# The last product of a ternary feed forward: float32 operands replaced by two float32r halves

## The chip, the cores and the metric

The kernel runs on one NeuronCore of a Trainium2 chip. The time is the device time of one execution in microseconds (us). Before the change three executions took 3924.77, 3930.02 and 3933.33 us; the median is 3930.02 us. The engines are named as in the profile: PE (TensorE, matrix products; PEld are its weight loads), DVE (VectorE), ACT (ScalarE), POOL (GpSimd) and SP, which issues DMAs.

## The reference

The kernel computes a decoder of four layers, each an attention, a second attention and a feed forward, with a layer normalisation after each, on 16 sequences of 128 tokens and width 256. The change touches one of the twelve stages, the feed forward of the third layer:

```python
def ternary_matmul(x, w):
    return jnp.matmul(x, jnp.sign(w).T)
xq = activation_quant(rms_norm(x))
g = jax.nn.silu(ternary_matmul(xq, W_g))
u = ternary_matmul(xq, W_u)
p = g * u
return ternary_matmul(p, W_d)
```

The hidden width is 1024. Only the signs of the weights enter, so each is -1, 0 or 1. The quantised input is a small integer and is exact in bfloat16. The gated values `p` are general float32 numbers; the product of `p` with the signs of `W_d` (the down product) is what changes. The stage before it (stage 7) is an attention without weights between the tokens and a context of the same sequence.

## The kernel before

The activations stay in the core's on-chip memory (`X`, 128 tokens by 16 sequences by 256). Stage 7 and stage 8 run woven into one another. `s7` makes 16 attention units, one for a sequence (`width_unit`), and 8 feed-forward pairs, one for two sequences (`s8_pair`). Both are generators, cut into pieces at each `yield`. `weave` goes through steps n and in each calls, in a fixed list, the next piece of the unit of sequence n - lag. In the list, A is the attention unit and B the pair:

```python
(A, 0), (A, 4), (A, 1), (A, 3), (A, 1), (A, 3), (A, 2), (A, 4), (B, 11), (B, 7),
(B, 8), (B, 6), (A, 1), (B, 5), (B, 9), (A, 2), (B, 13),
```

A pair belongs to two sequences and is called for both, so it advances 14 pieces: the statistics of `X` (on DVE, then `rs_ve` and `ln_rs` on POOL), the variance and normalisation, the quantisation, the transposes, four pieces with two chunks of 128 hidden columns each (c = 0, 2, 4, 6), two pieces with the down product of one sequence (j = 0 and j = 1), the statistics of the output, its normalisation on POOL, and its transposes. Worked out from the list: in an odd step come, in this order, the statistics of the output of the pair before, the transposes of the next pair, chunks 6 of a pair, chunks 0 of the next pair, the third piece of an attention unit (`xp`), the input statistics of the pair after next, and then the down product of j = 0. The attention piece with the products `xp,e` and the exponentials `e` follows it. In an even step come chunks 2 and 4 of one pair and the down product of j = 1 of the pair before it.

`Ordered` wraps the four compute engines while the stages are woven: each instruction is held behind the one that the code put before it on the same engine. So every engine's queue has the order of the list, and an instruction that waits holds all that stands behind it on its engine. All these instructions are recorded with the one line 324; they are told apart by their tiles.

A piece of two chunks makes eight bfloat16 products of the signs `sgu` with the quantised input `qT` into two banks, multiplies the gate's bank by the row scales (`t`, DVE), applies silu (`t`, ACT) and multiplies by the other bank (`h`, DVE). The buffer `hT` (tag `h8`, line 2153) holds the eight chunks of a pair in float32 and has two copies, since the next pair begins its chunks before the down product of this pair is done. The down product of j takes, for c from 0 to 7, the 128x128 block of `hT` as weights and the signs `d` of `W_d` (128x256, float32) as the moving side. Its result is scaled and added to `X` on DVE (`X<-bankB,rs,X`).

The banks of TensorE's results come from two rotating pools in this stage: six for the wide ones (`bankA`) and two for the others (`bankB`). ACT changes its function table between silu and the exponentials, once each way in a step (ACT_TABLE_LOAD).

Of the kernel before, what the change touches and what calls it, by code (L numbers as in the profile page):

```python
# [11 lines left out]

F32 = mybir.dt.float32
BF16 = mybir.dt.bfloat16
I32 = mybir.dt.int32
AF = mybir.ActivationFunctionType
ALU = mybir.AluOpType
# [5 lines left out]
D = 256  # L23
# [245 lines left out]
def bc(ap, *shape):  # L269
    return ap.to_broadcast(list(shape))  # L270
# [56 lines left out]
class Decoder:  # L327
# [47 lines left out]
    def setup(self):  # L375
# [15 lines left out]
        self.spare = self.const(base, "spare", nc.scalar)  # L391
        self.identb = base.tile([128, 128], BF16, name="identb")
        nc.vector.tensor_copy(self.identb, self.ident)
# [1236 lines left out]
    def w5(self, pool):  # L1630
        nc = self.nc
        w = {"gu_i": pool.tile([128, 2, 2, 704], I32, name="gu5i")}
        nc.sync.dma_start(w["gu_i"], self.a["s5_wgu"].rearrange("(k p) m h -> p k m h", p=128))
        w["d_i"] = pool.tile([128, 6, D], I32, name="d5i")
        nc.sync.dma_start(
# [63 lines left out]
    def s6(self, wk, w, last):  # L1699
        nc = self.nc  # L1700
        one = dict(bufs=1)
        w["neg"] = wk.tile([128, 128], BF16, name="neg6", **one)
        nc.vector.tensor_copy(w["neg"], w["neg_causal"])
# [372 lines left out]
    def quantise(self, wk, src, tag):  # L2076
# [8 lines left out]
        nc.vector.tensor_scalar(s, s, 127.0, None, ALU.mult)  # L2085
        q = wk.tile([128, n, m], BF16, tag="q" + tag, name="q" + tag)
        for j in range(n):
# [5 lines left out]
    def s8_signs(self, wk, w):  # L2093
        w["s"] = wk.tile([128, 2, 2, 1024], BF16, name="sgu8", bufs=1)
        self.nc.scalar.activation(w["s"], w["gu"], AF.Sign)
        self.nc.scalar.activation(w["d"], w["d"], AF.Sign)

    def s8(self, wk, w, last):

# [7 lines left out]
    def s8_pair(self, wk, w, b, last, norm=True):  # L2107

        nc = self.nc
        xs = self.X[:, b : b + 2, :]
        mv, rstd = self.moments([xs[:, j, :] for j in range(2)], 1e-5 if norm else 1e-8, "ln")
        yield
        var = self.sm(2, tag="var8")
        if norm:
            nc.gpsimd.tensor_tensor(var, mv[:, :2, 1], rstd[:, :2], ALU.mult)
            nc.gpsimd.tensor_tensor(var, var, rstd[:, :2], ALU.mult)
            self.rsqrt(var, var, 1e-8, 2)
            xh = xs  # L2120
        else:
            nc.gpsimd.memset(var, 1.0)
            xh = wk.tile([128, 2, D], F32, tag="xh8", name="xh8", bufs=1)
        for j in range(2):
            nc.vector.tensor_scalar(
                xh[:, j, :], xs[:, j, :], mv[:, j, 0:1], rstd[:, j : j + 1], ALU.subtract, ALU.mult
            )
        yield
        am, s, rs = (self.sm(2, tag=n + "8") for n in ("am", "s", "rs"))
        nc.vector.tensor_reduce(am, xh, AX.X, ALU.max, apply_absolute_value=True)  # L2130
        nc.vector.reciprocal(s, am)
        nc.vector.tensor_scalar(s, s, 127.0, None, ALU.mult)
        q = wk.tile([128, 2, D], BF16, tag="q8", name="q8", bufs=1)
        t = wk.tile([128, 2, D], F32, tag="t8", name="t8", bufs=1)
        for j in range(2):
            nc.vector.tensor_scalar(t[:, j, :], xh[:, j, :], s[:, j : j + 1], MAGIC, ALU.mult, ALU.add)
            nc.gpsimd.tensor_scalar(q[:, j, :], t[:, j, :], MAGIC, None, ALU.subtract)
        nc.gpsimd.tensor_scalar(am, am, 1.0 / 127.0, None, ALU.mult)
        nc.gpsimd.tensor_tensor(rs, am, var, ALU.mult)
        yield  # L2140
        p = self.pt(2, 2, 128, dtype=BF16)
        for j in range(2):
            for k in range(2):
                nc.tensor.transpose(p[:, k, j, :], q[:, j, 128 * k : 128 * k + 128], self.identb)
        qT = wk.tile([128, 2, 256], BF16, tag="qT8", name="qT8")
        nc.scalar.copy(qT, p.rearrange("p k j t -> p k (j t)"))
        p = self.pt(2, 128)
        for j in range(2):
            self.mm(p[:, j, :], bc(rs[:, j : j + 1], 128, 128), self.ident)
        rsb = wk.tile([128, 256], F32, tag="rsb8", name="rsb8")  # L2150
        nc.scalar.copy(rsb, p.rearrange("p j t -> p (j t)"))
        yield
        hT = wk.tile([128, 8, 256], F32, tag="h8", name="h8")
        for c in range(0, 8, 2):
            ps = [self.ps(2, 256) for _ in range(2)]
            for m in range(2):
                for i in range(2):
                    cs = slice(128 * (c + i), 128 * (c + i) + 128)
                    for k in range(2):
                        self.mm(ps[m][:, i, :], w["s"][:, k, m, cs], qT[:, k, :], k, 2)  # L2160
            t = wk.tile([128, 2, 256], F32, tag="t28", name="t28")
            nc.vector.tensor_tensor(t, ps[0], bc(rsb.unsqueeze(1), 128, 2, 256), ALU.mult)
            nc.scalar.activation(t, t, AF.Silu)
            nc.vector.tensor_tensor(hT[:, c : c + 2, :], ps[1], t, ALU.mult)
            yield
        for j in range(2):
            p = self.pt(D)
            for c in range(8):
                self.mm(p, hT[:, c, 128 * j : 128 * j + 128], w["d"][:, c, :], c, 8)
            nc.vector.scalar_tensor_tensor(  # L2170
                xs[:, j, :], p, rs[:, j : j + 1], xs[:, j, :], ALU.mult, ALU.add
            )
            yield
        mv, rstd = self.moments([xs[:, j, :] for j in range(2)], 1e-5, "ln")
        yield
        for j in range(2):
            nc.gpsimd.tensor_scalar(
                xs[:, j, :], xs[:, j, :], mv[:, j, 0:1], rstd[:, j : j + 1], ALU.subtract, ALU.mult
            )
        if last:  # L2180
            nc.sync.dma_start(self.out.rearrange("b s d -> s b d")[:, b : b + 2, :], xs)
        else:
            yield
            self.load_transposed(b // 4, [b // 2 % 2])
# [399 lines left out]
```

## Time and profile before

| | |
|---|---|
| median of three executions | 3930.02 us |
| span of the profiled execution, first to last instruction | 3927.2 us |
| the profiled execution's own time outside the span | not on the page; the median stands 2.8 us above the span |
| PE busy in the span | 3561.2 us (91%) |
| DVE, ACT, POOL busy | 2528.1 us (64%), 2076.7 us (53%), 1965.7 us (50%) |
| stretch of stages 7 and 8 | about 2362 to 2665 us, 303 us |
| PE, DVE, ACT, POOL busy in that stretch | 263.9, 191.0, 145.5, 112.0 us |
| mean granted TensorE clock over the span | 0.950 |

Busy times are unions of the recorded durations. A matrix product is recorded longer than the distance to the next one, because products overlap in the array; the distance between starts tells what one costs in a row of them. A float32 product is recorded as two MATMUL instructions, a bfloat16 product as one. `[1.42 <-DVE t L324]` behind a line says that the engine was idle for 1.42 us before it and that the instruction that wrote `t` on DVE ended the wait.

### The profile page before, as it was taken

How to read it: one execution, taken by the hardware profiler on the slowest of the kernel's cores; microseconds unless marked ns; L12 is line 12 of the kernel's file. 1: busy time of each engine (PE TensorE's matmuls, PEld its weight loads, DVE VectorE, ACT ScalarE, POOL GpSimd, SP SyncE). 2: the span in 40 equal slices, each digit the busy share in tenths (PEclk: the TensorE clock that was granted, in tenths of full speed). 3: DMA queues.
4: the chain of work that ended last, by engine and by line, in shares of the span. 5: the costliest groups of instructions: out<-in, count | busy, mean ns of one | idle time of the engine just before them, and what ended most of it. 6: DMA issues, size and time to landing. Idle time of an engine off the chain costs nothing.

```text
span 3927.2 us, 96527 instructions
## 1 busy us (share of the span) xinstructions
PE 3561.2 (91%) x39282; PEld 2164.1 (55%) x39282; DVE 2528.1 (64%) x5489; ACT 2076.7 (53%) x4583; POOL 1965.7 (50%) x2227
## 2 busy tenths in 40 slices
PE   6999999999999837798989998988999999999896
PEld 4666566666666524565545664665455454555453
DVE  3776667768767565566235556755666677666697
ACT  2666666666666513343115444544656565566386
POOL 1444444435434316652125552343886666676567
PEclk8999999999999968899979998998999999999898
DMA  2111111111111101100010003111111111111221
GB/s 88 35 38 37 35 37 38 36 36 37 37 35 33 37 0 47 42 12 16 1 57 30 27 24 110 52 48 46 36 42 37 36 42 36 41 38 40 74 68 33
DMA packets 120841, 156.47 MB, mean 40 GB/s; under 512 B 15632, under 2 KB 79888, under 8 KB 120016
## 3 DMA queue, kind: packets, MB, share of 16 engines
q1 hardware_dynamic: 114544, 143.59, 12.0%
q8 instruction: 311, 5.10, 0.6%
q10 hardware_dynamic: 5712, 5.19, 0.4%
q0 software_dynamic: 144, 1.52, 0.1%
q14 instruction: 130, 1.06, 0.1%
HBM read 131.64 MB, written 2.10 MB: 34 GB/s over the span
## 4 chain that ended last, share of the span: by engine, by line
PE 73%; DVE 12%; ACT 6%; POOL 5%; issue 3%; DMA 1%; SPq 0%; ACTq 0%; POOLq 0%; DVEq 0%
PE bankA L324 39%; PE bankB L324 20%; PE bankC L324 8%; PE bankA L465 3%; DVE npad L324 2%; PE bankB L465 2%; ACT accq L324 1%; ACT ot L324 1%; ACT gT L324 1%; POOL var L324 1%; DVE X L324 1%; DVE ln_st L324 1%; POOL t L324 1%; DVE t L324 0%; DVE accq L324 0%
## 5 line engine op out<-in xcount | busy, mean ns | idle before, releaser
L324 PE MATMUL bankA<-xT,wzx 128*128 128x512 f32 x1024 | 458.1, 600 | 0.0
L324 DVE SCALAR_TENSOR_TENSOR acc<-bankA,half,acc 128x508 f32<-128x508 f32 (+2 forms) x384 | 285.2, 743 | 167.2 <-ACT acc L324 158.2
L324 POOL TENSOR_TENSOR m<-m,gm 128x512 f32<-128x512 f32 x256 | 317.9, 1277 | 48.0 <-ACT m L324 48.0
L324 PEld LDWEIGHTS bankA<-xT,wzx 128*128 128x128 f32 x1024 | 190.1, 191 | 226.6 <-issue 188.4
L324 POOL TENSOR_TENSOR eb<-eb,c_tri_s 128x512 f32<-128x512 f32 x64 | 81.2, 1269 | 371.5 <-ACT eb L324 371.5
L324 POOL TENSOR_TENSOR gT<-yx,sz 128x512 f32<-128x512 f32 x128 | 160.5, 1275 | 211.4 <-DVE yx L324 211.4
L324 PE MATMUL bankA<-xT,wkq 128*128 128x512 f32 x512 | 259.1, 631 | 0.0
L324 PE MATMUL bankA<-xT,wvg 128*128 128x512 f32 x512 | 247.5, 606 | 0.1
L324 PE MATMUL bankC<-gT,wo 128*128 128x512 f32 x512 | 231.9, 596 | 2.7 <-POOL gT L324 2.7
L324 DVE TENSOR_REDUCE npad<-bankA 128x2 f32<-128x512 f32 (+1 forms) x320 | 196.9, 681 | 37.6 <-PE bankA L324 29.0
L324 ACT ACTIVATE m<-bankA 128x512 f32<-128x512 f32 x256 | 132.1, 604 | 157.4 <-PE bankA L324 157.4
L324 ACT ACTIVATE e<-bankA 128x512 f32<-128x512 f32 x320 | 165.2, 603 | 82.2 <-PE bankA L324 81.7
L324 POOL TENSOR_TENSOR sq<-sq,s 128x512 f32<-128x512 f32 x124 | 157.5, 1271 | 56.6 <-ACT s L324 51.9
L324 POOL TENSOR_SCALAR rs_ve<-o_mv 128x4 f32<-128x4 f32 x64 | 31.5, 492 | 298.9 <-DVE o_mv L324 289.6
L324 DVE SCALAR_TENSOR_TENSOR vT<-th,accv 128x512 f32<-128x512 f32 x64 | 45.4, 710 | 182.1 <-ACT th L324 182.1
L324 PEld LDWEIGHTS bankB<-y,tt 32*32 32x32 f32 x8192 | 87.5, 107 | 129.1 <-issue 93.7
L324 DVE SCALAR_TENSOR_TENSOR yx<-xs,cols,bankB 128x512 f32<-128x512 f32 x128 | 95.0, 747 | 90.2 <-PE bankB L324 84.5
L324 DVE SCALAR_TENSOR_TENSOR acck<-bankA,half_cols,acck 128x508 f32<-128x508 f32 (+2 forms) x192 | 142.5, 742 | 11.3 <-ACT acck L324 4.8
L324 PEld LDWEIGHTS bankC<-gT,wo 128*128 128x128 f32 x512 | 93.4, 192 | 98.4 <-issue 93.5
L324 DVE SCALAR_TENSOR_TENSOR accq<-bankA,half_cols,accq 128x508 f32<-128x508 f32 (+2 forms) x192 | 142.2, 740 | 4.5
L324 ACT ACTIVATE acc<-bankA,half 128x512 f32<-128x512 f32 x128 | 100.7, 786 | 80.0 <-PE bankA L324 80.0
L324 DVE SCALAR_TENSOR_TENSOR accv<-bankA,half_cols,accv 128x508 f32<-128x508 f32 (+2 forms) x192 | 140.0, 729 | 4.5
(528 smaller groups left out, 9375.9 us busy)
## 6 DMA issues: line engine op xcount, KB each, us to landing
wzx<-in_s_wzx SPq DMA_DIRECT2D x64, 512.0 KB
up<-cums SPq DMA_DIRECT2D x1152, 2.0 KB
wkq<-in_s_w SPq DMA_DIRECT2D x64, 256.0 KB
wvg<-in_s_w SPq DMA_DIRECT2D x64, 256.0 KB
wo<-in_s_wo SPq DMA_DIRECT2D x64, 128.0 KB
sw<-qraw SPq DMA_DIRECT2D x64, 128.0 KB
eo<-in_ctx_eo SPq DMA_DIRECT2D x32, 256.0 KB
e<-in_ctx_e SPq DMA_DIRECT2D x32, 256.0 KB
```

The costliest lines, as they stand in the source:

```text
L324: return lambda *a, **k: self.tc.keep_in_program_order(f(*a, **k))
L465: self.nc.tensor.matmul(out, lhsT=lhsT, rhs=rhs, start=(k == 0), stop=(k == n - 1))
```

## The change

The gated values are no longer kept as one float32 tile. Each piece now writes its two chunks into a small float32 tile (`h8`, 128x2x256, two copies). A new function `halve` makes two float32r tiles of it: ACT copies the chunk into `hh8`, which rounds it to that format, and POOL subtracts the copy from the chunk and writes the difference into `hl8`, rounded too. `hh8` and `hl8` hold the eight chunks of a pair and have one copy each. The halving of a piece's chunks is called in the next piece of the pair, between the silu and the DVE product; that of chunks 6 is called at the beginning of the piece with the down product of j = 0. The signs of the down weights are written into a new float32r tile `dr8` instead of in place. The down product of j becomes 16 products instead of eight: for each c the block of `hh8` and then the block of `hl8`, each with `dr8`, all summed in one bank.

```diff
+F32R = mybir.dt.float32r
...
-        self.nc.scalar.activation(w["d"], w["d"], AF.Sign)
+        w["dr"] = wk.tile([128, 8, D], F32R, name="dr8", bufs=1)
+        self.nc.scalar.activation(w["dr"], w["d"], AF.Sign)
...
-        hT = wk.tile([128, 8, 256], F32, tag="h8", name="h8")
+        hh, hl = (wk.tile([128, 8, 256], F32R, tag=n, name=n, bufs=1) for n in ("hh8", "hl8"))
+
+        def halve(c, h):
+            nc.scalar.copy(hh[:, c : c + 2, :], h)
+            nc.gpsimd.tensor_tensor(hl[:, c : c + 2, :], h, hh[:, c : c + 2, :].bitcast(F32), ALU.subtract)
+
+        h = None
         for c in range(0, 8, 2):
...
             nc.scalar.activation(t, t, AF.Silu)
-            nc.vector.tensor_tensor(hT[:, c : c + 2, :], ps[1], t, ALU.mult)
+            if c:
+                halve(c - 2, h)
+            h = wk.tile([128, 2, 256], F32, tag="h8", name="h8")
+            nc.vector.tensor_tensor(h, ps[1], t, ALU.mult)
             yield
+        halve(6, h)
         for j in range(2):
             p = self.pt(D)
             for c in range(8):
-                self.mm(p, hT[:, c, 128 * j : 128 * j + 128], w["d"][:, c, :], c, 8)
+                for i, part in enumerate((hh, hl)):
+                    self.mm(p, part[:, c, 128 * j : 128 * j + 128], w["dr"][:, c, :], 2 * c + i, 16)
```

## The prediction

> **What bounds the kernel now.** Read first: the page's shares and chain, for how much of the whole is at stake; then the groups of the stretch 2362 to 2665 us, where the feed forward runs; then the order of instructions in one odd and one even step; last the granted clock where TensorE sat idle.
>
> ```profile
> PE 73%; DVE 12%; ACT 6%; POOL 5%; issue 3%; DMA 1%; SPq 0%; ACTq 0%; POOLq 0%; DVEq 0%
> ...
> L324 POOL TENSOR_TENSOR m<-m,gm 128x512 f32<-128x512 f32 x256 | 317.9, 1277 | 48.0 <-ACT m L324 48.0
> ```
>
> The chain that ended last is mostly TensorE, so cheaper products look like time. The second line is of another stage: it prices a POOL operation on two 128x512 tiles.
>
> ```profile
> L324 PE MATMUL bankB<-d,h 128*128 128x256 f32 x256 | 59.0, 383 | 0.0
> ...
> L324 PE MATMUL bankA<-qT,sgu 128*128 128x256 bf16 x256 | 33.9, 290 | 0.2 <-ACT qT L324 0.2
> ...
> L324 ACT ACTIVATE t<-t 128x512 f32<-128x512 f32 x32 | 20.2, 630 | 28.3 <-DVE t L324 28.2
> ```
>
> Groups of the stretch (busy us, mean ns | idle before). The down products are 128 in the code and 256 records: two per float32 product. They are some 55 of the stretch's 303 us.
>
> An odd step (columns: start, us, engine, operation, number, idle before and who ended it):
>
> ```profile
> 2467.94 3.62 PE L324 MATMUL bankB<-d,h 128*128 128x256 f32 x16
> 2468.46 0.63 ACT L324 ACTIVATE t<-t 128x512 f32<-128x512 f32 x1
> 2469.12 0.69 DVE L324 TENSOR_TENSOR h<-bankA,t 128x512 f32<-128x512 f32 x1 [2.03 <-ACT t L324]
> ...
> 2470.51 0.63 ACT L324 ACTIVATE t<-t 128x512 f32<-128x512 f32 x1 [1.42 <-DVE t L324]
> ...
> 2471.49 1.15 PE L324 MATMUL bankA<-xp,e 32*128 32x256 f32 x16
> ...
> 2473.22 0.30 DVE L324 BATCH_NORM_AGGREGATE ln_mv<-ln_st 128x2 f32<-128x6 f32 x2
> ...
> 2473.61 0.22 POOL L324 TENSOR_SCALAR rs_ve<-ln_mv 128x2 f32<-128x2 f32 x1 [6.84 <-DVE ln_mv L324]
> ...
> 2473.92 0.73 POOL L324 TENSOR_TENSOR ln_rs<-rs_ve,c_neghalf 128x2 f32<-128x2 f32 x1
> ```
>
> TensorE starts the first down half (j=0) before its last chunk is written (2469.81) and reads that chunk late, so it never stops. POOL waits 6.84 us for statistics that come after the chunk.
>
> An even step:
>
> ```profile
> 2512.78 3.62 PE L324 MATMUL bankB<-d,h 128*128 128x256 f32 x16
> 2513.10 2.43 POOL L324 TENSOR_SCALAR X<-X,ln_mv,ln_rs 128x256 f32<-128x256 f32 x2
> ...
> 2515.51 0.63 ACT L324 ACTIVATE t<-t 128x512 f32<-128x512 f32 x1 [1.42 <-DVE t L324]
> 2516.16 1.28 ACT L324 ACT_TABLE_LOAD   x1
> 2516.17 0.69 DVE L324 TENSOR_TENSOR h<-bankA,t 128x512 f32<-128x512 f32 x1 [0.76 <-ACT t L324]
> ...
> 2517.49 2.06 ACT L324 ACTIVATE e<-bankA 128x512 f32<-128x512 f32 x4
> ...
> 2520.38 1.07 PE L324 MATMUL bankB<-e,vp 128*32 128x256 f32 x16 [0.25 <-DVE X L324]
> ```
>
> Here the silu chain (ACT, DVE in turn) decides: the exponentials begin when the table is loaded (2517.44), and TensorE waits for DVE's update of X.
>
> The clock (stretch and length; PE busy and count, then PEld, DVE, ACT, POOL; granted clock):
>
> ```profile
> 2606.83:2610.24 3.41, 0.00 (x0) 0.00 (x0) 2.02 (x8) 0.00 (x0) 1.87 (x4) 1.00 0.00 0
> 2610.24:2613.66 3.42, 2.24 (x10) 1.61 (x11) 1.28 (x4) 0.58 (x1) 1.87 (x4) 0.50 0.00 0
> 2613.66:2617.07 3.41, 3.41 (x18) 2.53 (x17) 1.19 (x5) 1.90 (x3) 1.89 (x4) 0.50 0.31 73
> ```
>
> After 3.41 us without TensorE work the next two slices are granted half the clock.
>
> **The products.** Sixteen records in 3.62 us, the last 0.38 long, start (3.62 - 0.38)/15 = 0.216 us apart, so a j costs 16 x 0.216 = 3.46. No float32r is in the trace. Lower bound: the bfloat16 rows of the same 128x256 (16 in 1.91 us, the last 0.27) are 0.109 apart. Upper bounds: the spacing of a float32 record, 0.216, or of a whole float32 product, 0.431. I take 0.108, since one record with one reading of 256 columns is nearest to the bfloat16 row. A j is 16 x 0.108 = 1.73: 1.73 less, 27.7 us over 16 j.
>
> [...] This trace's bfloat16 loads are recorded beside matmuls over the same rows, at 0.109 spacing.
>
> **The halves.** Per pair, four ACT copies of 128x512 (0.63, the silu row, also an SBUF to SBUF pass) and four POOL subtracts (1.28, the m row; two of the stage's own 128x256 additions would be 1.46). That is 20 us of ACT and 41 us of POOL over eight pairs. What matters is their place in queues that run in the order of the code.
>
> **Odd step.** The last chunk's copy is written behind the next pair's first silu: 2471.14, and it ends at 2471.78. Its subtract would follow at once, but in POOL's queue the statistics of the pair after next (rs_ve, ln_rs) stand before it. ln_rs ends at 2474.65, so the subtract runs 2474.66 to 2475.94. TensorE has by then done everything but the last low part of chunks 6 and what follows: three products, 0.32, so xp,e starts at 2476.32, not 2471.49: 4.83 later. Chunks 4 and 5 make shorter waits inside that (copy to 2469.72, subtract to about 2471.1, which is just before the DVE product of 2471.17 reuses that chunk's buffer). Queued behind: xp,e, then ACT's four exponentials, the o transposes, the next eo. About 0.6 comes back, since the X update that those transposes need is done while xp,e runs; it was 1.9 us behind the products. Net 4.2.
>
> **The clock in that gap.** Between 2471.9 and 2476.0 TensorE has nothing to do, longer than the 3.41 us slice above, and it is thinly used for 2 us before. From the two rows at 0.50 I take one slice at half clock overlapping work that matters: 3.41 x 0.5 = 1.7 us. Bounds: 0 (the slice falls in the wait) and 3.4 (two slices of work).
>
> [...]
>
> **Even step.** The j=1 products end 1.73 earlier, near 2514.7, which frees nothing: exponentials wait for the table load. New: hh8 has one buffer, so the next pair's first copy waits for these products: 2514.73 to 2515.36, before the silu at 2515.51, free. h8 has two buffers of one chunk: the DVE product of 2516.17 needs the subtract of two chunks before to be over. POOL is in the normalisation until 2515.53, the subtract ends 2516.82, DVE goes at 2516.87: 0.7 later, and all of DVE up to the X update that TensorE awaits at 2520.38. The second copy lies between silu and table load: 0.63, parallel to that 0.7. I take 0.7. POOL's next work (var) moves by 2.6 but has until the next odd step.
>
> **The rest.** The sign of the down weights goes to a new tile, one ACTIVATE of 1.89 us as before: nothing. No DMA is added or moved. In the last two pairs no statistics of a later pair stand in front; there POOL's own normalisations and subtracts eat what the products give. I take 0, bounds -7 (4 x 1.73) and +5 (two more POOL pairs of subtracts).
>
> **Sum.** Six odd steps with later statistics (pairs 0 to 5): 6 x (4.2 + 1.7) = 35.4. Six even steps: 6 x 0.7 = 4.2. Together 39.6 us on the profiled span of 3927.2, whose kernel runs at 3930.02 in the median, 2.8 above the span: 3970.
>
> **The rivals.**
> - The wait is shorter: the statistics are not what the subtract waits behind. Then it ends at 2473.1, xp,e starts 1.98 later, less 0.6, no clock loss: 6 x 1.4 + 4.2 = 12.6, 3943. For: copy and subtract alone are that short. Against: all POOL instructions go through the wrapper that keeps program order.
> - Products cost 0.216. Then j=1 ends at 2516.5, the first copy holds the silu of 2515.51 by 1.7 (9.6 more over six even steps), odd steps lose 0.32 more (2) and the end 3.5: 15 more, 3985. At 0.431 the j=1 products alone are 3.4 longer than now: about 4022.
> - Faster: the last subtract is done when its product comes. Then 1.73 a j counts in six odd steps and the last pairs, 6 x 1.73 + 7 = 17: 3913. It decides at 2471.2: a subtract over by then leaves xp,e where it is. But the chunk is written at 2469.81 and copy plus subtract take 1.91, so even without a queue it is 0.5 late; only a different order of the queues gives it.
> - The stall falls into slack and nothing shows: 3930. Against: TensorE is busy 18 to 19 us in every 20 from 2440 to 2560.
>
> **How the numbers follow.** The forecast 0.62 (3955 to 3985 its own range), shorter wait 0.13, costlier products 0.16, faster 0.05, no change 0.04. The range runs from the shorter wait, 3943, to costlier products with part of a second half-clock slice, 3996; outside lie faster and no change (0.09), and 0.431 or more (some 0.06). A measurement here tells 0.2%, 8 us, from nothing. Faster 0.05, within 0.04, slower 0.91.
>
> **What would show it.** Down records: 256 still, one per product and half, 0.108 apart where not waiting, with a gap of 3 to 4 us before the last three of each odd j; POOL's subtract after ln_rs; the stretch from the first eo to the next stage near 340 us, not 303; slices of 0.5 clock between 2470 and 2600. Wrong: no gap there, subtracts before the statistics, or records 0.2 apart or more.

## The result and the profile after

The changed kernel takes 3984.64 us in the median (3979.28 to 3990.91, four executions) against 3928.49 us (3924.77 to 3933.33, four executions) of the kernel before: a ratio of 1.0139, 95% interval 1.0127 to 1.0151. It is 56 us slower; the forecast was 40 slower (3970), in a range of 3943 to 3996. The profiled span went from 3927.2 to 3987.8 us and the mean granted clock from 0.950 to 0.937. Everything is now recorded with line 325.

The page of the changed kernel has these lines for the two that were shown first, the chain that ended last by engine and the POOL row of another stage:

```profile
PE 25%; DVE 5%; POOL 1%; issue 1%; ACT 1%; ACTq 0%; POOLq 0%; DVEq 0%
...
L325 POOL TENSOR_TENSOR m<-m,gm 128x512 f32<-128x512 f32 x256 | 317.8, 1275 | 45.7 <-ACT m L325 45.7
```

The chain accounts for a third of the span here, so its shares can't be set beside those of before; the POOL operation costs what it did. Next the groups of the woven stretch after the change (busy us, mean ns of one | idle before it and what ended that idle time):

```profile
L325 POOL TENSOR_TENSOR hl<-h,hh 128x512 fp32r<-128x512 f32 x32 | 40.2, 1267 | 30.9 <-ACT hh L325 28.5 <-DVE t L325 2.4
L325 PE MATMUL bankB<-dr,hh 128*128 128x256 f32 x128 | 38.3, 323 | 7.8 <-ACT hh L325 7.0
L325 PE MATMUL bankB<-dr,hl 128*128 128x256 f32 x128 | 38.1, 325 | 30.1 <-POOL hl L325 30.1
...
L325 ACT CAST hh<-h 128x512 fp32r<-128x512 f32 x32 | 19.4, 606 | 8.1 <-PE bankB L325 7.7 <-DVE h L325 0.3
```

The down products were 256 records with an idle time of 0.0 in front of them; now they are 128 of the high and 128 of the low half, and TensorE stands 30 us in front of low halves, waiting for POOL's subtract. Busy time of the product is no help here: the mean record lasts 323 ns, but the records overlap and start 0.12 us apart where they don't wait. The distance between starts is the cost.

An odd step of the changed kernel (columns: start, us, engine, line, operation, number, idle before and who ended it):

```profile
2515.76 0.60 ACT L325 CAST hh<-h 128x512 fp32r<-128x512 f32 x1
2515.94 0.69 DVE L325 TENSOR_TENSOR h<-bankA,t 128x512 f32<-128x512 f32 x1 [2.09 <-ACT t L325]
...
2517.86 0.60 ACT L325 CAST hh<-h 128x512 fp32r<-128x512 f32 x1
...
2520.48 0.23 POOL L325 TENSOR_SCALAR rs_ve<-ln_mv 128x2 f32<-128x2 f32 x1 [2.78 <-DVE ln_mv L325]
2520.80 0.71 POOL L325 TENSOR_TENSOR ln_rs<-rs_ve,c_neghalf 128x2 f32<-128x2 f32 x1
2521.48 1.26 POOL L325 TENSOR_TENSOR hl<-h,hh 128x512 fp32r<-128x512 f32 x1
2522.80 0.58 PE L325 MATMUL bankB<-dr,hl 128*128 128x256 f32 x1 [3.90 <-POOL hl L325]
...
2523.74 2.09 PE L325 MATMUL bankA<-xp,e 32*128 32x256 f32 x16
...
2525.84 1.58 ACT L325 ACTIVATE e<-bankA 128x512 f32<-128x512 f32 x3 [6.08 <-PE bankA L325]
```

The copy of the last chunks is over at 2518.46. POOL is idle and could subtract, but it waits 2.78 us for the statistics `ln_mv`, computes `rs_ve` and `ln_rs`, and subtracts only then. TensorE waits 3.90 us, and `xp,e`, which took 1.15 us, takes 2.09.

The reason for the 2.09 is in the next view: three stretches of that step (start:end and length; busy PE, PEld, DVE, ACT, POOL, each with its count; the granted clock; DMA).

```profile
2518.00:2521.40 3.40, 0.76 (x4) 0.36 (x3) 2.35 (x7) 1.74 (x2) 0.84 (x2) 0.96 0.00 0
2521.40:2524.80 3.40, 2.00 (x15) 1.63 (x19) 0.48 (x1) 0.00 (x0) 1.34 (x2) 0.50 0.00 0
2524.80:2528.20 3.40, 3.40 (x24) 1.70 (x16) 0.28 (x2) 2.06 (x4) 0.98 (x2) 0.54 0.25 77
```

TensorE was busy for 0.76 of 3.40 us, and the two stretches after it ran at about half the clock (0.50 and 0.54), though the second was full of work.

Two lines of an even step before the change, which the prediction didn't show:

```profile
2516.78 0.72 DVE L324 TENSOR_SCALAR X<-X,ln_mv,ln_rs 128x256 f32<-128x256 f32 x2
...
2518.43 0.63 PE L324 MATMUL bankB<-c_ident,o 128*128 128x128 f32 x4 [0.95 <-DVE xp L324]
```

And the same place after it:

```profile
2538.02 0.62 ACT L325 CAST hh<-h 128x512 fp32r<-128x512 f32 x1 [0.74 <-PE bankB L325]
...
2538.72 2.49 POOL L325 TENSOR_TENSOR hl<-h,hh 128x512 fp32r<-128x512 f32 x2
...
2540.02 0.69 DVE L325 TENSOR_TENSOR h<-bankA,t 128x512 f32<-128x512 f32 x1 [1.37 <-POOL hl L325]
2540.63 1.05 DVE L325 TENSOR_SCALAR X<-X,ln_mv,ln_rs 128x256 f32<-128x256 f32 x2
...
2541.60 0.86 DVE L325 SCALAR_TENSOR_TENSOR xp<-X,c_parity,bankB 128x256 f32<-128x256 f32 x2
...
2542.61 1.09 PE L325 MATMUL bankB<-c_ident,o 128*128 128x128 f32 x4 [3.37 <-DVE xp L325]
```

DVE's product now waits for POOL, as forecast. Two things were not forecast: the normalisation behind it (`TENSOR_SCALAR X`) went from 0.72 to 1.05 us, and TensorE's idle time before the transposes of `o` went from 0.95 to 3.37 us. Those transposes then take 1.09 instead of 0.63: a second gap in every pair of steps, with half-clock slices of its own (0.50 granted from 2541.6 to 2548.4 us).

The readings that follow are by steps. An odd step is the time from the first down record of j=0 to that of j=1 of a pair, an even step the time from there to the next pair's j=0. Before the change the six odd steps were 14.14, 14.14, 15.22, 15.21, 10.84 and 5.64 us, the even ones 16.57, 16.56, 16.55, 14.28, 15.88 and 13.11. Each row below adds up by how much a kernel's steps are longer than these, in its profiled execution. "Ends" are the four intervals of the last two pairs, the last of them up to the third and last copy of the transposed output on ACT (`xT<-bankB`) after that product. The last column sets the median against that of the kernel before, measured beside it (3928.49 to 3935.04 us).

| kernel | six odd | six even | ends | sum | median minus before |
|---|---|---|---|---|---|
| the change | +40.8 | +12.9 | +4.0 | +57.6 | +56.2 |
| subtract before the statistics | +20.7 | +12.1 | +2.5 | +35.3 | +31.3 |
| last chunks halved early | +10.1 | +9.5 | +2.2 | +21.8 | +16.5 |
| four `h8` buffers | +40.7 | +12.9 | +2.2 | +55.8 | +51.3 |
| zero products in the odd gap | +29.6 | +10.8 | +2.7 | +43.1 | +43.6 |
| high halves alone | +2.2 | +6.2 | -5.1 | +3.3 | +2.2 |
| early, half of the subtracts | +13.1 | +3.0 | +1.4 | +17.6 | +15.6 |
| halves for half of the chunks | +0.2 | +3.9 | -1.9 | +2.1 | +0.1 |
| early, zero products after j=1 | +12.3 | +9.3 | +3.7 | +25.3 | +21.5 |
| the same, half of the subtracts | +11.4 | +1.3 | +3.1 | +15.8 | +9.5 |

The sums are of one execution each and differ from the medians by up to 6 us. Before the first odd step the profiled executions differ by up to 17 us: it begins at 2467.9 before the change, at 2473.6 after it, and between 2463.6 and 2481.1 in the experiments. Four buffers, whose steps equal those of the change, begin 10 us earlier. So most of the +5.7 there belongs to the execution: 4.3 us of it are there at the first product with `sgu` (2439.1 and 2443.4). The other 1.4 come between that product and the first odd step, where the first pair is halved: 28.8 us before, 30.3 with the change and with four buffers, 28.8 again in the kernels without the subtracts of chunks 0 to 3. They are the change's own and stand in no row of the table.

### The profile page after: what moved, and what is told of

It is laid out like the page before. It is cut to its first block, busy times and chain, and to the rows that moved or that the text cites. A ratio compares the mean times of both kernels' runs of the same rounds, so it can differ in the third digit from the quotient of the medians.

```text
span 3987.8 us, 96595 instructions
## 1 busy us (share of the span) xinstructions
PE 3579.6 (90%) x39282; PEld 2172.9 (54%) x39282; DVE 2532.0 (63%) x5489; ACT 2093.6 (52%) x4615; POOL 2005.8 (50%) x2259
## 3 DMA queue, kind: packets, MB, share of 16 engines
q14 instruction: 130, 1.06, 0.1%
```

## The experiments

Theory: POOL's queue order costs the odd steps, a buffer wait the even ones, and each gap of TensorE lowers its clock. The rivals were that the order does not matter, that the work of halving itself costs the time, and that the products do.

**The subtract before the statistics.** One call of the feed-forward pair changes its place in the list of the weave, so that the last subtract is issued before the input statistics.

```diff
-(B, 8), (B, 6), (A, 1), (B, 5), (B, 9), (A, 2), (B, 13),
+(B, 8), (B, 6), (A, 1), (B, 9), (B, 5), (A, 2), (B, 13),
```

> One thing changes: in the list the j=0 product is called before the input statistics of the pair after next, so the last subtract stands in front of rs_ve and ln_rs in POOL's queue. Theory (the subtract waits in POOL's queue behind statistics that come late): it begins when the copy ends, xp,e starts about 2.0 us later than in the kernel before, not 4.8, the gap of 3.9 us before the last three products falls to 1.2, and the half-clock slices behind odd steps go. Odd steps are some 4.8 us shorter than in the changed kernel, six of them: about 3956 us. Rival (the products, the copies or the buffers cost the time): the odd steps stay as they are, 3980 to 3990 us.

Measured: 3961.66 us, ratio 1.0087 [1.0064, 1.0109]. Odd steps of the kernel with the swapped order:

```profile
2521.23 0.60 ACT L325 CAST hh<-h 128x512 fp32r<-128x512 f32 x1
...
2521.91 1.27 POOL L325 TENSOR_TENSOR hl<-h,hh 128x512 fp32r<-128x512 f32 x1 [0.84 <-ACT hh L325]
...
2523.23 0.38 PE L325 MATMUL bankB<-dr,hl 128*128 128x256 f32 x1 [0.96 <-POOL hl L325]
...
2523.77 1.74 PE L325 MATMUL bankA<-xp,e 32*128 32x256 f32 x16
```

The subtract now follows its copy at once, and TensorE's wait falls from 3.90 to 0.96 us. The first odd step is 3.4 us longer than before instead of 7.1. Its slices at half clock go from two to one; the expectation had none left, and 4.8 us a step where 3.4 were gained. Nothing but the order changed: the place in the queue, with the slice that its gap brings, is half of the odd loss. The even steps stayed where they were.

**The last chunks halved early.** The call `halve(6, h)` moves from the next piece of the pair into the piece that writes `h`.

```diff
             nc.vector.tensor_tensor(h, ps[1], t, ALU.mult)
+            if c == 6:
+                halve(6, h)
             yield
-        halve(6, h)
```

> One thing changes: the halves of the last two chunks are made in the piece that computes them, right after the DVE product, two places earlier in the list than the j=0 product. Theory: the copy comes before the next pair's silu (about 1.9 to 2.6 us after j=0 starts), the subtract directly behind that of chunks 4, and the last three products wait for it until 4.5 us after the start, xp,e 1.3 us later than in the kernel before. Odd steps 5.5 us shorter than in the changed kernel: about 3952 us; even steps still 3 us longer than before. Rival (the cost of the subtract itself, 1.27 us, bounds the step wherever it stands): POOL ends later, 3970 us or more.

Measured: 3946.94 us, 1.0037 [1.0023, 1.0051]. In an odd step POOL now subtracts chunks 4 and 6 in a row, and TensorE waits 0.50 us before the last three products instead of 3.90:

```profile
2507.24 2.51 POOL L325 TENSOR_TENSOR hl<-h,hh 128x512 fp32r<-128x512 f32 x2 [1.78 <-ACT hh L325]
...
2509.81 0.39 PE L325 MATMUL bankB<-dr,hl 128*128 128x256 f32 x1 [0.50 <-POOL hl L325]
```

The first four odd steps are 1.3, 1.3, 0.4 and 0.4 us longer than before, with no slice at half clock in any of them; the first four even ones are 2.1 to 2.3 longer and have one slice of 3.4 us each, where the change has two. One early call takes the loss from 56.2 to 16.5 us. What remains is about as much in the odd steps (+10.1) as in the even ones (+9.5). Of the odd part 6.8 us are in the last two of the six, which have a half-clock slice each; the rest of their loss was not followed up.

**Four `h8` buffers.** This takes away what the product of DVE waits for in an even step.

```diff
-            h = wk.tile([128, 2, 256], F32, tag="h8", name="h8")
+            h = wk.tile([128, 2, 256], F32, tag="h8", name="h8", bufs=4)
```

> One thing changes: the small float32 chunk tile has four buffers instead of two, so a DVE product no longer waits for the subtract of two chunks before. Theory for the even steps (this wait makes DVE late, which leaves TensorE idle before the o transposes and costs clock): DVE's second product goes 0.7 us earlier, the gap of 3.4 us before the o transposes falls to 2.7, fewer half-clock slices; even steps 1 to 2 us shorter, about 3974 us. Rival (the second ACT copy in front of the table load, or the shorter products alone, make the even step longer): even steps as they are, 3982 to 3987 us. Odd steps unchanged by both.

Measured: 3981.68 us, 1.0136 [1.0119, 1.0153], and each of the twelve steps as long as with the change. Even step with four buffers:

```profile
2528.73 2.49 POOL L325 TENSOR_TENSOR hl<-h,hh 128x512 fp32r<-128x512 f32 x2
...
2529.36 0.69 DVE L325 TENSOR_TENSOR h<-bankA,t 128x512 f32<-128x512 f32 x1 [0.75 <-POOL X L325]
...
2529.97 1.73 DVE L325 TENSOR_SCALAR X<-X,ln_mv,ln_rs 128x256 f32<-128x256 f32 x2
```

The wait of the product is gone: it starts 0.63 after the subtracts begin, not 1.30. But the normalisation behind it now takes 1.73 us, not 1.05, and DVE comes to `xp` at the same distance from the subtracts. In the trace's records the first of the two TENSOR_SCALAR lasts 1.40 us in place of 0.40 and ends 0.15 us after POOL's second subtract; with the change it lasts 0.73 and ends at the same 0.15. So the buffer was one of two ties between DVE and POOL, and the other holds when the first is cut: this DVE operation on SBUF tiles is held while POOL runs its subtract. By what it is held, no run here shows. The theory of the buffer alone fell here.

**Zero products in the odd gap.** Thirty products with zero weights between the high and the low half of chunk 6, in j=0 of the pairs before the last two. They add nothing to the sum and are to hold the clock.

```diff
+        w["zr"] = wk.tile([128, 128], F32R, name="zr8", bufs=1)
+        self.nc.scalar.activation(w["zr"], w["d"][:, 0, :128], AF.Copy, scale=0.0)
...
                 for i, part in enumerate((hh, hl)):
                     self.mm(p, part[:, c, 128 * j : 128 * j + 128], w["dr"][:, c, :], 2 * c + i, 16)
+                    if (j, c, i) == (0, 6, 0) and b < 12:
+                        for _ in range(30):
+                            self.mm(p, w["zr"], w["dr"][:, c, :], 1, 16)
```

> Added: in the j=0 product of the first six pairs, 30 products of a tile of zeros with the same signs between the high and the low half of chunk 6, summed into the same bank, where they add nothing. At 0.12 us each they fill 3.6 of the 3.9 us in which TensorE waits for the subtract. Theory (part of an odd step's 6.8 us is the half clock granted after that wait): the clock stays at 1.0 behind odd steps, the wait for the subtract stays, each odd step is about 1.7 us shorter, 3974 us in all. Rival (the half clock falls into slack): 3985 us, no change. If the fillers delay the last three products, it is slower than that.

Measured: 3973.96 us, 1.0121 [1.0097, 1.0146]. Odd step with the zero products:

```profile
2514.04 3.76 PE L325 MATMUL bankB<-dr,zr 128*128 128x256 f32 x30
...
2516.79 1.28 POOL L325 TENSOR_TENSOR hl<-h,hh 128x512 fp32r<-128x512 f32 x1
2518.12 0.39 PE L325 MATMUL bankB<-dr,hl 128*128 128x256 f32 x1 [0.33 <-POOL hl L325]
...
2518.67 1.15 PE L325 MATMUL bankA<-xp,e 32*128 32x256 f32 x16
```

The subtract ends as late as with the change (6.83 us after the start of the DVE product of chunks 6, there 6.80), but `xp,e` is back at 1.15 us. The six odd steps lose 29.6 us instead of 40.8: the clock's share was 11.2 us, 1.9 a step, and the rest 4.9 a step (the sixth still had 4.4 us at half clock). So added work shortens the steps. In the whole time the medians fall by 12.6 us, but the two intervals overlap, so the gain rests on the steps.

**High halves alone.** DVE writes the high half directly, there is no copy and no subtract, and a j has eight products. This bounds what cheaper products can give.

```diff
...
-            if c:
-                halve(c - 2, h)
-            h = wk.tile([128, 2, 256], F32, tag="h8", name="h8")
-            nc.vector.tensor_tensor(h, ps[1], t, ALU.mult)
+            nc.vector.tensor_tensor(hh[:, c : c + 2, :], ps[1], t, ALU.mult)
...
-                for i, part in enumerate((hh, hl)):
-                    self.mm(p, part[:, c, 128 * j : 128 * j + 128], w["dr"][:, c, :], 2 * c + i, 16)
+                self.mm(p, hh[:, c, 128 * j : 128 * j + 128], w["dr"][:, c, :], c, 8)
```

> Only the high halves: DVE writes the gated values straight into a float32r tile with two buffers, there is no copy, no subtract, and a down product has 8 products of 0.12 us instead of 16 records of 0.216. The low halves are left out, so the result is less exact. Theory (beside the attention the ACT and DVE chain sets the step, not the time of the products): odd steps gain at most 0.6 us each, since the exponentials still wait for the table load, even steps nothing, the last two pairs up to 2.5 us per product: 3915 to 3927 us. Rival (TensorE-bound, a saved us of product is a saved us): 16 x (3.46 - 0.96) = 40 us less than before, 3890 us.

Measured: 3933.82 us, 1.0008 [0.9999, 1.0016]. Eight products take some 0.96 us instead of 3.46, 40 us of TensorE less over 16 j, and the kernel is not faster at all. That is above the theory's 3927 as well as the rival's 3890: the theory had left out the clock. The transposes of `o` in an odd step before the change, and in an odd and an even step of this kernel:

```profile
2472.79 0.63 PE L324 MATMUL bankB<-c_ident,o 128*128 128x128 f32 x4
...
2501.01 0.63 PE L325 MATMUL bankB<-c_ident,o 128*128 128x128 f32 x4 [1.34 <-DVE xp L325]
...
2515.85 1.09 PE L325 MATMUL bankB<-c_ident,o 128*128 128x128 f32 x4 [2.44 <-DVE xp L325]
```

In the odd step they start 3.66 us after the start of the DVE product of chunks 6, against 3.67 before: where TensorE went from product to product it now waits 1.34 us for `xp`. In the even step they start when `xp` is done, as they did before; the time saved in the products turned into 1.5 us more idle time before them, and the clock went to half (they take 1.09 us instead of 0.63). Odd steps without a half-clock slice are 0 to 0.2 us shorter than before, those with one 1.3 longer; the first even step, with one slice, is 1.0 longer and the second, with two, 2.4. Only the last two pairs gain, 5.1 us.

**Early, half of the subtracts.** The early kernel with the subtracts of chunks 0 to 3 left out, so that their low halves are missing from the result; chunks 2 and 3 are those whose subtract stands beside the normalisation in an even step.

```diff
-            nc.gpsimd.tensor_tensor(hl[:, c : c + 2, :], h, hh[:, c : c + 2, :].bitcast(F32), ALU.subtract)
+            if c >= 4:
+                nc.gpsimd.tensor_tensor(hl[:, c : c + 2, :], h, hh[:, c : c + 2, :].bitcast(F32), ALU.subtract)
...
-                for i, part in enumerate((hh, hl)):
+                for i, part in enumerate((hh, hl) if c >= 4 else (hh, hh)):
```

> As e2_early, but the subtracts of chunks 0 to 3 are left out (the high half is taken twice there, the number of products stays), so that in even steps POOL makes no subtract; the copies stay. Theory, after the four buffers changed nothing: in even steps DVE's normalisation of X cannot run while POOL's subtracts run (recorded 1.40 us instead of 0.40), so DVE, the xp pieces and the o transposes come late. Then the normalisation is back at 0.4 us, the gap before the o transposes falls from 3.4 to under 2 us, even steps lose some 1.5 us against e2_early: 3936 to 3940 us. Rival (the second ACT copy before the table load, or the shorter products, make the even steps longer): 3945 to 3949 us, as e2_early.

Measured: 3947.26 us, 1.0045 [1.0032, 1.0059], no faster than the early kernel, so by its time the rival holds. The steps tell more. The even steps without a half-clock slice are now 0.04 and 0.06 us from before, while half-clock slices appear in the second to fourth odd steps, which had none with the early call alone, and these are 1.9 to 2.6 longer. The cure moved the gaps, and the clock took back what the subtracts gave. The run alone could not separate the two; the last pair of runs does.

**Halves for half of the chunks.** Chunks 0, 1, 4 and 5 are halved, with the subtract on DVE, and 2, 3, 6 and 7 stay one float32 product each.

```diff
...
+            if c in (4, 6):
+                part = lo if c == 4 else hi
+                nc.vector.tensor_tensor(hl[:, part, :], h, hh[:, part, :].bitcast(F32), ALU.subtract)
...
+                if c in (0, 1, 4, 5):
+                    for i, part in enumerate((hh, hl)):
+                        self.mm(p, part[:, at, cols], w["dr"][:, c, :], c + i, 9)
+                else:
+                    self.mm(p, hf[:, at, cols], w["dr"][:, c, :].bitcast(F32), c + 1, 9)
```

> Another arrangement with the exact result: chunks 0, 1, 4, 5 are halved, chunks 2, 3, 6, 7 stay float32 (the float32r signs read as float32), the subtracts are on DVE, and copies and subtracts stand where ACT and DVE waited for something else in the kernel before (copy 0 behind the silu of chunks 2, copy 4 before the silu of chunks 6, the subtracts between t and h). A down product costs 8 x 0.12 + 4 x 0.431 = 2.7 us instead of 3.46. Theory (with the halves off the critical places nothing is lost, and nothing can be won beside the attention): 3922 to 3932 us, the same as before. Rival (any ACT or DVE work added to these chains costs its time): 0.6 to 1.3 us more in 12 steps, 3937 us or more.

Measured: 3931.76 us, 0.9997 [0.9987, 1.0007]: no difference from the kernel before. Its steps are as before but for two even ones with half-clock slices, +1.0 and +2.7. Halving can be hidden here; but there is no gain left to see.

**Zero products after j=1, with all subtracts and with half of them.** Fourteen products with zero weights behind the sixteen of each j=1 put back the TensorE time that the change saves there, and hold the clock in the even steps. The same edit goes onto the early kernel and onto the one with half of the subtracts.

```diff
...
-                    self.mm(p, part[:, c, 128 * j : 128 * j + 128], w["dr"][:, c, :], 2 * c + i, 16)
+                    self.mm(p, part[:, c, 128 * j : 128 * j + 128], w["dr"][:, c, :], 2 * c + i, 16 + 14 * j)
+            if j:
+                for n in range(16, 30):
+                    self.mm(p, w["zr"], w["dr"][:, n % 8, :], n, 30)
```

> The last chunk halved early, as before, and 14 products with zero weights (14 x 0.12 = 1.7 us of TensorE) behind the sixteen of each j=1; the result is unchanged. In the early kernel an even step was 2.1 us longer than before, with one slice of half clock in each. Theory (two causes: DVE's normalisation held by POOL's subtract, about 1.1, and the half-clock slice, about 1.0): with the clock held, even steps are 1.1 longer than before and no slice of 0.50 follows them; the whole comes to about 3941. Rival one (all of it is the clock): even steps within 0.2 of before, 3935. Rival two (all of it is the held normalisation): even steps stay at +2.1 with the clock held, 3947.

> The kernel without the subtracts of chunks 0 to 3 (their low halves are left out, the high half is multiplied twice), with the same 14 zero products behind each j=1. Theory of two causes: no subtract runs beside DVE's normalisation and the clock is held, so even steps are within 0.2 us of before, 1 below the same fillers with the subtracts; the whole about 3938 to 3942, since slices in odd steps may stay. If even steps show the same length with and without the subtracts, the held normalisation is worth nothing. If they are over 1 longer than before here too, the fillers delay something themselves.

Measured: 3956.52 us, 1.0061 [1.0043, 1.0079] with all subtracts, and 3944.56 us, 1.0027 [1.0015, 1.0039] with half of them (the kernel before took 3935.04 beside them). Even step with all subtracts:

```profile
2523.73 0.69 DVE L325 TENSOR_TENSOR h<-bankA,t 128x512 f32<-128x512 f32 x1 [1.39 <-POOL hl L325]
2524.34 1.06 DVE L325 TENSOR_SCALAR X<-X,ln_mv,ln_rs 128x256 f32<-128x256 f32 x2
...
2526.33 0.63 PE L325 MATMUL bankB<-c_ident,o 128*128 128x128 f32 x4 [1.84 <-DVE xp L325]
```

And with half of them:

```profile
2524.13 0.69 DVE L325 TENSOR_TENSOR h<-bankA,t 128x512 f32<-128x512 f32 x1 [0.76 <-ACT t L325]
...
2524.74 0.73 DVE L325 TENSOR_SCALAR X<-X,ln_mv,ln_rs 128x256 f32<-128x256 f32 x2
...
2526.39 0.63 PE L325 MATMUL bankB<-c_ident,o 128*128 128x128 f32 x4 [0.88 <-DVE xp L325]
```

The transposes of `o` take 0.63 us in both, as before the change at a granted clock of 1.00, so the clock is full. With all subtracts the first two even steps are 1.02 us longer than before, with half of them 0.06 and 0.07. That is the two ties to POOL, 1.0 us: the product waits 1.39 instead of 0.76 (0.63), and the normalisation takes 1.06 instead of 0.73 (0.33). The early kernel had 2.12 in these steps, so a half-clock slice was worth 1.1. By these steps both rivals are out. The totals missed their expectations, with all subtracts by far (3941) and with half of them a little (3938 to 3942): slices of half clock came up in odd steps, the first two of which are 2.5 longer with all subtracts where the early kernel had 1.3. The fillers moved the gaps against the slices rather than removing them.

## Why the prediction was right or wrong

The direction, the main mechanism and the range held; the size was 17 us short. Forecast +39.6, measured +56.2 in the medians, and +57.6 by the steps: odd steps +40.8 (forecast 35.4), even steps +12.9 (4.2), ends +4.0 (0). That 3985 is also the number of the rival with dearer products is chance: it had 0.216 us a product, and the profile has 0.12.

- **The products, 0.108 us.** Where they don't wait, records start 0.12 us apart: a j=1 runs from 2535.89 to its last start at 2537.76. A j costs about 1.9 instead of 1.73. The weight load of 0.19 us is recorded beside running products over the same rows and does not set that distance. The size hardly mattered: with half as many products (high halves alone) the six odd and the six even steps are together no shorter.
- **The halves.** 606 ns a copy and 1267 ns a subtract, against 0.63 and 1.28. Right.
- **Odd step, the queue.** From the DVE product of chunks 6 to the end of their subtract the prediction had 2475.94 - 2469.12 = 6.82 us; the profile has 2522.74 - 2515.94 = 6.80. The order as the cause is shown by the swap and by the early call. The net 4.2 was mis-sized: with the clock held it is 4.9. The 0.6 that was to come back did so only in the steps that were 15.2 us long before; those of 14.14 lose 5.1; why, no run shows.
- **Odd step, the clock.** One slice and 1.7 us were taken; two slices followed and cost 1.9, by the zero products. The size came out nearly right by luck: twice the slices, each at about half the price. Nor does the fall need 3.41 us without work, the gap that the prediction took for it: TensorE was busy for 0.76 us in the stretch before.
- **Even step, 0.7.** This is the step that failed. Of the ties to POOL it had the product's wait, 0.63 by the fillers, but not the longer normalisation, 0.33. And it said of the earlier end of j=1 that it "frees nothing", which is true of work, but it left out what the free time costs: TensorE idles 3.37 us instead of 0.95 before the transposes of `o`, and two slices at half clock follow, 2.1 us in the first two even steps (3.14 less 1.02). The last two even steps, which had 6.8 and 5.3 us of half clock before the change, lose only 0.4 and 0.6.
- **The ends, 0.** They cost 4.0 us, within the stated bounds of -7 and +5. The high halves alone gain 5.1 there, so halving and the eight low products of each j together cost some 9 us there.
- **What would show it.** The 256 records, the gap before the last three of an odd j (3.90 us) and POOL's subtract after `ln_rs` are there, as are the half-clock slices. The woven stretch ends 63 us later, not 37, by the terms above and the later start.
- **The rivals.** A shorter wait and dearer products are out by the odd step's lines and by the 0.12 us (in the sum of the latter, six waits of 1.7 us are 10.2, not 9.6), no change by the +56.2. The faster case, 3913, counted 1.73 us a j as gain once the subtract is in time. The high halves alone have more gain and no halving at all, and are not faster: the six odd steps have no such gain in them. What bounds these steps, too, is the chain of silu and DVE work that the prediction named for even steps alone: with the high halves alone TensorE waits for its `xp`, and before the change the products were just as late. TensorE's large share in the chain of waits "looks like time" and was not.

## What to carry to other kernels

Work that is added to an engine with idle time costs by its place in that engine's queue: before pricing its duration, list what it will stand behind and what that in turn waits for. One call moved to an earlier piece took the loss from 56 to 17 us here. Time taken off TensorE inside a stage that another chain sets was no gain here (a ratio of 1.0008 with the high halves alone), and was a loss in the steps where the idle time lowered the clock of the work behind it (up to 2.4 us in a step of the high halves alone).

## What was not expected of the hardware

- A DVE `tensor_scalar` from SBUF to SBUF that takes 0.40 us by itself was held beside POOL's subtract until 0.15 us after that operation's end: to 0.73 us with the change, to 1.40 with four buffers.
- An idle TensorE cost time after the gap, too: in the steps above one slice at half clock was worth 1.0 to 1.3 us, two 1.9 to 2.4. Zero products in the gap gave 11 us back over six odd steps; in another place they moved the slices into other steps.
- The gap was not always a whole slice long. In the traces before and after the change every stretch at one granted clock, but the last, is a whole number of slices of 3.413 us. In the feed-forward steps of the eleven traces, taken by these slices, all 68 full-clock slices with TensorE busy for less than 0.45 of the time were followed by one at half clock, and none of the 388 with more than 0.7 was; in between it was 28 of 89.
